# A gated linear-attention block: the Hadamard transform of gate's and up's input moved from the weights to the tokens

## The chip, the cores and the metric

One Trainium2 chip, one of its cores. The core has five engines that run beside each other, each in its own order: TensorE (PE, matmuls), VectorE (DVE), ScalarE (ACT), GpSimd (POOL) and SyncE (SP, which in this kernel issues nearly all DMAs). They meet through semaphores. The metric is the device time of one launch in microseconds; less is better. A profile is one execution taken by the hardware profiler; its times can be followed instruction by instruction.

## The reference

Input x is 8 batch elements of 512 tokens by 512 features, float32. Cut to what is computed:

```python
xn = layernorm(x)
# attention: q, k, v by 512x512 weights with bias; phi = elu + 1
ctx = phi(q) * cumsum(phi(k) * v, over tokens) / sqrt(32)
s   = ctx @ Wo.T + bo
# feed-forward, hidden size 2048; fwht = normalized Walsh-Hadamard transform
h   = fwht(xn * SU_ug) / 64
up, gate = (h @ W.T * (Wscale * 64) for W in (W_up, W_gate))
h   = fwht(silu(gate) * up * SU_dp) / 64
d   = h @ W_down.T * (Wscale_dp * 64)
out = x + s * silu(d)
```

The transform of a vector of 512 can be applied to the input, as written, or to the columns of the weights, which then take xn itself.

## The kernel before

**Tiles and pairs.** The eight batch elements are taken in four pairs p = 0 to 3. A pair's product is split by two in rows of the weights, in columns and in batch elements, and done with seven products of blocks instead of eight (`P1` to `P7`, a Strassen-like scheme): the tokens, the weights and the results each have seven "factors" or blocks. For pairs 1 to 3, gate and up are computed with two levels of the scheme (49 products of quarter blocks, `hidden_unit` and `block_product`), on second-level weight factors that pair 0 stored to DRAM (`inner_w`).

**Stages of a pair.** `attention` (k, v, q in two groups of heads), then four units u of the hidden layer (gate and up for 512 hidden columns, result `ho`), with the output projection `project_out` after unit 0; `down` in two halves, half 0 after unit 1, half 1 after unit 3. Half 0 writes its sums to tiles `dn` and stores them (`put_by`); half 1 fetches them and adds its own, gates, multiplies and writes out. `down` goes through `token_groups`: two groups g of tokens, products P1 and P7 first, then P2 (bank py), P6, P5, P3, P4. The sums of P2 for group 0 must be read by DVE (`output`, line 543) before P2 of group 1 can use the only `py` bank.

**Weights of gate and up.** In pair 0, `folded_w` (lines 919 to 955) loads a raw weight tile, runs four butterflies on DVE (lines 930 to 933), two matmuls with the 128x128 Hadamard matrix `had` on PE (line 939), scales by SU_ug on ACT while copying back (line 945), and forms the factors (`encode_weights`). There are 16 such tiles. Down's weights get their transform in the same pair: `butterflies_down`, `fold_down`, and then `first_half_down` for half 0, with `down_w` for half 1.

**Tokens.** Pair 0's tokens are normalized and transposed by PE (`transposed`) into `xo`, which holds the first-level factors of the pair. For later pairs, `normalized` normalizes an element by token on DVE during the pair before and stores it (`d_x`); `next_tokens` reads it back as 32x32 squares (`squares`), turns the squares with DVE's transpose, and forms the factors. `inner_tokens` and `inner_t3` add the second-level factors to the same `xo`, which attention, gate and up all use.

**What sets the order.** `at(place, fn)` puts a step on an agenda counted in places (one product of TensorE each); `advance` runs it. `later(us, fn)` puts work of DVE on a list, and `pace` issues entries of it behind each sum on DVE, up to a number of microseconds. `background` lowers the priority. A scheduler then fixes one order for each engine, and each engine, SP too, goes through its own strictly in order: an instruction that waits holds up everything behind it on that engine. Weights are streamed three tiles ahead through a pool of four (`wpool`); working tiles share a pool of six (`t8`), `ho` and `co` a pool of two (`hop`).

Of the kernel before, what the change touches and what calls it, by code (L numbers as in the profile page):

```python
# [10 lines left out]
ALU = mybir.AluOpType  # L11
# [10 lines left out]
def kernel(  # L22
# [26 lines left out]

    nc = tc.nc  # L50
# [14 lines left out]
    hop = ctx.enter_context(tc.tile_pool(name="hop", bufs=2))  # L65
# [53 lines left out]
    su_ug = const.tile([P, KD], F32, tag="su_ug", name="su_ug")  # L119
# [3 lines left out]
    def load_x(b, t=None, parts=1):  # L123
        if t is None:
            t = xin.tile([P, 3, 7, P], F32, tag="x", name=f"x_{b}")
            t = t.rearrange("p c s e -> p (c s e)")[:, : NT * D].rearrange("p (n d) -> p n d", n=NT)
        n = NT // parts
        for i in range(0, NT, n):
            nc.sync.dma_start(
                t[:, i : i + n], x[b, i * P : (i + n) * P, :].rearrange("(n p) d -> p n d", p=P)  # L130
            )
        return t
# [48 lines left out]


    def normalized(b):

        xt = load_x(b)
        d = dram.tile([L, D], F32, tag=f"d_x_{b}", name=f"d_x_{b}")
        kept[f"x_{b}"] = d

        def store():
            nc.sync.dma_start(d.rearrange("(n p) d -> p n d", p=P), xt)  # L190

        if b > 3:
            layernorm(b, xt)
            store()
            return
        mv = small.tile([P, NT, 2], F32, tag="mv", name=f"mv_{b}")
        rstd = small.tile([P, NT], F32, tag="rstd", name=f"rstd_{b}")

# [15 lines left out]

        def start():
            for t in range(NT):
                later(0.8, stats, t)
            later(0.3, root)
            for t in range(NT):
                later(0.6, scaled, t)  # L220
            later(0.0, store)

        at(12, start)

    def squares(b):


        if b % 2:
            z = t8.tile([P, KD, L], F32, tag="t", name=f"z_{b}")
        else:  # L230
            z = xin.tile([P, 3, 7, P], F32, tag="x", name=f"z_{b}")
            z = z.rearrange("p c s e -> p (c s e)")[:, : KD * L].rearrange("p (c t) -> p c t", c=KD)
        d = kept[f"x_{b}"].rearrange("(i t) (c j f) -> j t c i f", t=32, j=4, f=32)
# [4 lines left out]
    def next_tokens(b, xo):  # L238

        za, z = squares(b), squares(b + 1)  # L240

        def turned(place, z, h):

            for j in range(2):
                later(0.7, nc.vector.transpose, xo[:, place, j : j + 3 : 2, :], z[:, 2 * h + j])

        def less(o, a, b):
            later(1.2, nc.vector.tensor_tensor, xo[:, o, 0:4], xo[:, a, 0:4], xo[:, b, 0:4], ALU.subtract)

        turned(P1, za, 0)  # L250
        turned(P2, za, 1)

        def rest():
            turned(P7, z, 0)
            turned(P3, z, 1)
            less(P5, P7, P1)
            less(P6, P3, P5)
            less(P7, P3, P7)
            less(P4, P2, P6)

        at(10, rest)

# [3 lines left out]
    def transposed(b, xt, xo):  # L266
        s = b % 2
        for t in range(NT):
# [7 lines left out]
            else:  # L276
# [4 lines left out]
                nc.vector.tensor_tensor(o[:, P7], o[:, P3], b12, ALU.subtract)  # L281
        if s == 1:
            o = xo[:, :, 0:4]
            nc.vector.tensor_tensor(o[:, P4], o[:, P2], o[:, P6], ALU.subtract)

    def inner_tokens(xo):

        for o, a, b in ((P5, P7, P1), (P6, P3, P5), (P4, P2, P6)):
            later(2.0, nc.vector.tensor_tensor, xo[:, :, o], xo[:, :, a], xo[:, :, b], ALU.subtract)

    def inner_t3(xo, factors):
        for i in factors:
            nc.vector.tensor_tensor(xo[:, i, P7], xo[:, i, P3], xo[:, i, P7], ALU.subtract)
# [80 lines left out]
    def down_w(u, j):  # L374

        t = t8.tile([P, 2, 7, P], F32, tag="t", name=f"wd_{u}_{j}")
        w = by_factor(t)
        rows_w(w, wd_f, u + NU * j, NG)

        def encode():  # L380
            for o, a, b, op in (
                (P5, P7, P4, ALU.add), (P6, P5, P1, ALU.subtract), (P3, P2, P6, ALU.subtract), (P7, P1, P7, ALU.subtract)
            ):
                later(0.5, nc.vector.tensor_tensor, w[:, o], w[:, a], w[:, b], op)
            later(0.0, store)
# [56 lines left out]
    def group(name, ws, rhs, dst, then, bias=(None, None)):  # L442
# [24 lines left out]
        def output(i, s, p):  # L467
            pace(nc.vector.tensor_tensor(dst[i], s, p.rearrange("p a t -> p (a t)"), ALU.add), 1.7)  # L468
# [43 lines left out]
    def token_groups(name, n, tok, wts, dst, add=None, early=None, done=None, last=None):  # L512
# [29 lines left out]
        def output(o, p, a, s, g):  # L542
            pace(nc.vector.tensor_tensor(dst(a, s, g), o, p, ALU.add), 1.0)  # L543
# [78 lines left out]
    def block_product(name, w, x, out, add, done):  # L622
# [5 lines left out]
        def product(p, i, first):  # L628
            for lane in range(2):
                nc.tensor.matmul(  # L630
                    p[:, lane], w[:, lane, i, :], x[:, i, :],
# [171 lines left out]
    def hidden_unit(p, u, xo, ho, get_w, last):  # L803
# [4 lines left out]
        def outer(i, out, add=None, done=None):  # L808
            w = get_w("gu", (u, i))
            block_product(f"gu_{p}_{u}_{i}", w, xo[:, i], out, add, done)  # L810
# [108 lines left out]
    def folded_w(name, src, f):  # L919

        w = raw_w(f"{name}_{f}", src, 0, 2, 1, f * P, NG * P)
        places = (slice(P1, P7 + 1, 2), slice(P2, P4 + 1, 3))
        rs = []

        def butterflies():
            t = t8.tile([P, 2, 2, 2, 2, P], F32, tag="t", name=f"r_{name}_{f}")
            r2, r = t[:, 0], t[:, 1]
            rs.append(r)
            a, b = (w[:, :, place, :] for place in places)
            nc.vector.tensor_tensor(r2[:, 0], a, b, ALU.add)  # L930
            nc.vector.tensor_tensor(r2[:, 1], a, b, ALU.subtract)
            nc.vector.tensor_tensor(r[:, :, 0], r2[:, :, 0], r2[:, :, 1], ALU.add)
            nc.vector.tensor_tensor(r[:, :, 1], r2[:, :, 0], r2[:, :, 1], ALU.subtract)

        def fold():
            for b in range(2):
# [316 lines left out]
```

## Time and profile before

| | us |
|---|---|
| median of 3 runs (lowest, highest) | 1569.39 (1566.1, 1570.06) |
| the profiled execution's own time | 1565.26 |
| its span, first to last instruction | 1563.5 |
| PE busy in the stretches 0:50, 50:100, 100:200 | 41.8, 46.6, 92.0 |
| PE busy in 200:300, 300:400, 400:500 | 98.7, 96.8, 95.9 |
| PE busy in each 100 us from 500 to 1500 | 100.0 |
| DVE busy in 50:100, 100:200, 200:300 | 48.9, 81.9, 54.8 |
| DMA, mean share of 16 engines on the one queue | 51.8% |

Pair 0 takes the first 460 us or so, the other three some 365 each. "Busy" of an engine is the time in which it ran an instruction; matmuls overlap, so two that follow each other are closer than the duration of one. Rows of the timeline give start, duration, engine, line, operation, output and inputs, size and count, and in brackets how long the engine had been idle and what ended that.

### The profile page before, as it was taken

Reading aid. Unit: us, or ns where it says so; the run is one execution under the profiler, and the core shown is the slowest. Engines: PE = TensorE matmul, PEld = TensorE weight load, DVE = VectorE, ACT = ScalarE, POOL = GpSimd, SP = SyncE. Lnnn points to the kernel's source line nnn. Section 1 sums busy time; section 2 is a strip of 40 time slices with the busy share of each in tenths; the row PEclk is TensorE's granted clock in tenths of the full one; section 3 lists DMA queues with packets and bytes.
Section 4 is the critical chain, followed back from the end, with each engine's and each line's share of the span. In section 5 each row is a group of like instructions: output and inputs, shape, how many; then the busy total and the mean of one; then the engine's idle time right before and its main releaser. Section 6 shows DMA issues by size and latency. Waiting matters only on the chain.

```text
span 1563.5 us, 15520 instructions
## 1 busy us (share of the span) xinstructions
PE 1529.6 (98%) x5840; PEld 1105.7 (71%) x5840; DVE 953.9 (61%) x1336; ACT 419.8 (27%) x666; POOL 501.5 (32%) x286
## 2 busy tenths in 40 slices
PE   7989999999999999999999999999999999999998
PEld 4335546744584588888885488888886468888887
DVE  5898784469466674716676574725675476543673
ACT  5453340232114521112215431111212431111211
POOL 4532144014421252304612235301622226110731
PEclk9999999999999999999999999999999999999999
DMA  8244966566885344344575434335474233535462
GB/s 280 83 148 152 285 227 205 185 199 214 229 305 173 89 161 152 110 159 158 157 283 216 101 138 144 139 101 195 151 250 172 82 106 118 185 98 178 152 251 95
DMA packets 196682, 266.86 MB, mean 171 GB/s; under 512 B 56704, under 2 KB 155008, under 8 KB 192384
## 3 DMA queue, kind: packets, MB, share of 16 engines
q1 hardware_dynamic: 196464, 265.84, 51.8%
q8 instruction: 46, 0.75, 0.2%
q14 instruction: 28, 0.23, 0.0%
q10 hardware_dynamic: 144, 0.03, 0.0%
HBM read 189.83 MB, written 76.02 MB: 170 GB/s over the span
## 4 chain that ended last, share of the span: by engine, by line
PE 88%; DVE 4%; DMA 2%; POOL 2%; ACT 2%; issue 2%; SPq 0%; POOLq 0%; DVEq 0%; ACTq 0%
PE px_gu L630 19%; PE px_dn L528 13%; PE pz_gu L630 9%; PE pz_dn L528 6%; PE py_gu L630 5%; PE py_dn L528 4%; PE px_o L528 3%; PE px_up L452 3%; PE px_k L452 3%; PE px_v L452 3%; PE px_gate L452 3%; PE px_q L452 3%; PE pz_o L528 2%; PE pz_q L452 2%; PE pz_k L452 2%
## 5 line engine op out<-in xcount | busy, mean ns | idle before, releaser
L630 PE MATMUL px_gu<-xo,w_gu 128*128 128x256 f32 x1344 | 320.6, 380 | 0.0
L630 PEld LDWEIGHTS px_gu<-xo,w_gu 128*128 128x128 f32 x1344 | 254.7, 190 | 39.9 <-issue 3.6
L528 PE MATMUL px_dn<-w_down,ho 128*128 128x256 f32 x1024 | 228.5, 379 | 0.0
L528 PEld LDWEIGHTS px_dn<-w_down,ho 128*128 128x128 f32 x1024 | 194.5, 190 | 28.2 <-issue 2.1
L630 PE MATMUL pz_gu<-xo,w_gu 128*128 128x256 f32 x672 | 172.9, 380 | 0.0
L831 POOL TENSOR_TENSOR u<-u,v 128x1024 f32<-128x1024 f32 x24 | 56.1, 2359 | 354.2 <-DVE u L668 347.5
L630 PEld LDWEIGHTS pz_gu<-xo,w_gu 128*128 128x128 f32 x672 | 127.2, 190 | 18.4 <-DVE a L672 0.9
L528 PE MATMUL pz_dn<-w_down,ho 128*128 128x256 f32 x496 | 112.7, 380 | 2.7 <-POOL ho L300 2.7
L528 PEld LDWEIGHTS pz_dn<-w_down,ho 128*128 128x128 f32 x496 | 93.6, 190 | 17.9 <-POOL ho L300 3.5
L876 POOL TENSOR_TENSOR s<-s,d 128x512 f32<-128x512 f32 x30 | 40.4, 1346 | 152.8 <-ACT d L875 113.7
L716 POOL TENSOR_TENSOR v<-v,k 128x1024 f32<-128x1024 f32 x16 | 43.0, 2686 | 140.4 <-ACT v L691 112.7
L630 PE MATMUL py_gu<-xo,w_gu 128*128 128x256 f32 x336 | 86.2, 379 | 0.0
L630 PEld LDWEIGHTS py_gu<-xo,w_gu 128*128 128x128 f32 x336 | 63.9, 190 | 8.7
L793 POOL TENSOR_TENSOR ho<-g,u 128x512 f32<-128x512 f32 x8 | 12.5, 1557 | 164.6 <-DVE u L468 154.7
L835 POOL TENSOR_TENSOR v<-v,r 128x1024 f32<-128x1024 f32 x24 | 56.2, 2365 | 25.6 <-DVE r L668 25.6
L452 PE MATMUL px_v<-xo,w_v 128*128 128x512 f32 x128 | 60.8, 594 | 1.5 <-ACT sc_v L464 1.5
L875 ACT ACTIVATE d<-d 128x512 f32<-128x512 f32 x31 | 19.5, 630 | 158.3 <-DVE d L543 116.1
L452 PE MATMUL px_k<-xo,w_k 128*128 128x512 f32 x128 | 60.9, 597 | 1.1 <-ACT sa_k L464 1.0
L452 PE MATMUL px_gate<-xo,w_gate 128*128 128x512 f32 x128 | 59.7, 594 | 0.9 <-ACT sc_gate L462 0.9
L452 PE MATMUL px_q<-xo,w_q 128*128 128x512 f32 x128 | 60.1, 592 | 0.0
L452 PE MATMUL px_up<-xo,w_up 128*128 128x512 f32 x128 | 59.3, 592 | 0.0
L528 PE MATMUL px_o<-w_o,co 128*128 128x256 f32 x256 | 58.4, 379 | 0.0
(263 smaller groups left out, 2464.1 us busy)
## 6 DMA issues: line engine op xcount, KB each, us to landing
w_gu<-d_gu SPq DMA_DIRECT2D x84, 896.0 KB, 4.5
w_down<-d_down SPq DMA_DIRECT2D x56, 512.0 KB, 3.5
d_s<-o SPq DMA_DIRECT2D x8, 1024.0 KB, 4.4
d_d<-dn SPq DMA_DIRECT2D x8, 1024.0 KB, 7.6
d<-d_d SPq DMA_DIRECT2D x8, 1024.0 KB, 6.7
s<-d_s SPq DMA_DIRECT2D x8, 1024.0 KB, 7.9
y<-in_x_dram SPq DMA_DIRECT2D x8, 1024.0 KB, 7.8
out_dram<-y SPq DMA_DIRECT2D x15, 512.0 KB, 3.3
```

What stands on the lines that cost most here:

```text
L452: nc.tensor.matmul(p.rearrange("p a t -> p (a t)") if len(r.shape) == 2 else p, ws[k][:, i, :], r, start=(first and k == 0), stop=(k == n ...
L528: nc.tensor.matmul(p[:, c], t[:, (2 * g + c) * P : (2 * g + c + 1) * P], ws[i](k), start=(first and k == 0 and c == cs[0]), stop=(k == n - ...
L630: nc.tensor.matmul(p[:, lane], w[:, lane, i, :], x[:, i, :], start=(first and lane == 0), stop=True, skip_group_check=True,)
L716: nc.gpsimd.tensor_tensor(v[:, h], v[:, h], k[:, h], ALU.mult)
L793: nc.gpsimd.tensor_tensor(ho[:, P1], g[:, 0, 0], r[:, 0, 0], ALU.mult)
L831: nc.gpsimd.tensor_tensor(r[:, m], ru1[:, m], rv[:, m], ALU.add)
L835: nc.gpsimd.tensor_tensor(rv[:, m], rv[:, m], rr[:, m], ALU.add)
L875: nc.scalar.activation(d, d, AF.Silu)
L876: (nc.vector if final and (a, s) == (1, 0) else nc.gpsimd).tensor_tensor(r, r, d, ALU.mult)
```

## The change

Gate's and up's weights are no longer transformed. Their tiles are loaded raw and only get their factors (`hidden_w`). Instead there are two sets of tokens: plain ones for attention (`xa`) and transformed ones for gate and up (`xp`), each in a tile of `hop`, which has three now; the second-level factors move to a tile of their own (`xi`), whose space in pair 0 serves for down's weights (`rd`) and the scaled Hadamard matrices (`hads`).

- Pair 0: `first_transform` multiplies the factors of each of the two elements by `hads` on PE (four products), copies on ACT and does four butterflies on DVE.
- Pairs 1 to 3: `normalized` also stores the tokens times SU_ug (`times_scales`, POOL, then `d_xs`). In half 0 of down of the pair before, `transforms` reads both elements back and runs the full transform by token: nine levels of two steps (128x1024 each) for the odd element on DVE and for the even one on POOL (`transformed`), and stores the results (`d_xh`). During the next attention `hidden_tokens` reads them as squares, turns them and forms both levels of factors.
- The factor 1/sqrt(512) goes into gate's scale and `su_dp`; the preparation of down's weights starts two groups later; `first_half_down` uses `down_w`; the sums of down's half 0 release up to 5.0 us of listed work each instead of 1.0, those of `group` 2.2 instead of 1.7.

```diff
-    hop = ctx.enter_context(tc.tile_pool(name="hop", bufs=2))
+    hop = ctx.enter_context(tc.tile_pool(name="hop", bufs=3))
...
+    def normalized(b, delay=12):
+        t = xin.tile([P, 3, 7, P], F32, tag="x", name=f"x_{b}").rearrange("p c s e -> p (c s e)")
+        xt = t[:, : NT * D].rearrange("p (n d) -> p n d", n=NT)
+        su = t[:, NT * D : (NT + 1) * D]
+        load_x(b, xt)
+        nc.sync.dma_start(su, su_row.rearrange("o d -> (o d)").partition_broadcast(P))
...
+        def store():
+            put("x")
+            at(10, times_scales)
+        def times_scales():
+            for t in range(NT):
+                nc.gpsimd.tensor_tensor(xt[:, t], xt[:, t], su, ALU.mult)
+            put("xs")
...
+    def transformed(b, eng):
+        a, t = (t8.tile([P, NT, D], F32, tag="t", name=f"{n}_{b}") for n in ("xs", "xh"))
+        nc.sync.dma_start(a, kept[f"xs_{b}"].rearrange("(n p) d -> p n d", p=P))
+        d = dram.tile([L, D], F32, tag=f"d_xh_{b}", name=f"d_xh_{b}")
+        kept[f"xh_{b}"] = d
+        n = D.bit_length() - 1
+        def level(i, op):
+            x, y = ((a, t), (t, a))[i % 2]
+            x, y = (v.rearrange("p n (c t h) -> p (n c) t h", t=2, h=1 << i) for v in (x, y))
+            eng.tensor_tensor(y[:, :, op], x[:, :, 0], x[:, :, 1], (ALU.add, ALU.subtract)[op])
+            if i + 1 == n and op == 1:
+                nc.sync.dma_start(d.rearrange("(n p) d -> p n d", p=P), (a, t)[n % 2])
+        return [lambda i=i, op=op: level(i, op) for i in range(n) for op in range(2)]
...
+    def hidden_tokens(b, xp):
+        za = squares(f"xh_{b}", xin)
+        def first():
+            turned(xp, P1, za, 0)
+            turned(xp, P2, za, 1)
+            later(0.0, second)
+        def second():
+            z = squares(f"xh_{b + 1}", xin)
+            def rest():
+                turned(xp, P7, z, 0)
+                turned(xp, P3, z, 1)
+                outer_factors(xp)
+                inner_tokens(xp)
+            at(10, rest)
+        at(10, first)
...
+    def token_factors(name):
+        return new_h(name).rearrange("p m s t -> p (m s t)").rearrange("p (i n t) -> p i n t", i=7, n=4)
...
+    def first_transform(s, xa, xp):
+        t = t8.tile([P, KD, L], F32, tag="t", name=f"xh_{s}")
+        t2 = t8.tile([P, KD, L], F32, tag="t", name=f"xh2_{s}")
+        def product(c):
+            x = (xa[:, (P1, P2)[c // 2]] if s == 0 else (xp[:, P7], xa[:, P3])[c // 2])[:, c % 2 : c % 2 + 3 : 2, :]
+            p = ps.tile([P, 2, H], F32, tag="t", name=f"ph_{s}_{c}")
+            tc.keep_in_program_order(
+                nc.tensor.matmul(p, hads[:, c * P : (c + 1) * P], x, start=True, stop=True)
+            )
+            nc.scalar.copy(t[:, c], p.rearrange("p a t -> p (a t)"))
+        def butterflies():
+            places = slice(P1, P2 + 1) if s == 0 else slice(P7, P3 + 1)
+            u = t2.rearrange("p (h j) (i t) -> p j h i t", h=2, i=2)
+            for j, op in enumerate((ALU.add, ALU.subtract)):
+                later(1.2, nc.vector.tensor_tensor, t2[:, 2 * j : 2 * j + 2], t[:, 0:2], t[:, 2:4], op, soon=True)
+            for j, op in enumerate((ALU.add, ALU.subtract)):
+                later(1.2, nc.vector.tensor_tensor, xp[:, places, j : j + 3 : 2, :], u[:, 0], u[:, 1], op, soon=True)
+            if s == 1:
+                outer_factors(xp, soon=True)
+        for c in range(KD):
+            at(2 * c, lambda c=c: product(c))
+        at(2 * KD + 2, butterflies)
...
+    def inner_tokens(xp):
+        for o, a, b in (
+            (xi[:, :, P5 - P4], xp[:, :, P7], xp[:, :, P1]),
+            (xi[:, :, P6 - P4], xp[:, :, P3], xi[:, :, P5 - P4]),
+            (xi[:, :, 0], xp[:, :, P2], xi[:, :, P6 - P4]),
+            (xp[:, :, P7], xp[:, :, P3], xp[:, :, P7]),
+        ):
+            later(2.0, nc.vector.tensor_tensor, o, a, b, ALU.subtract)
...
+            pace(nc.vector.tensor_tensor(dst(a, s, g), o, p, ALU.add), 5.0 if n == 4 and add is None else 1.0)
...
-    def folded_w(name, src, f):
+    def hidden_w(name, src, f):
 
         w = raw_w(f"{name}_{f}", src, 0, 2, 1, f * P, NG * P)
-        places = (slice(P1, P7 + 1, 2), slice(P2, P4 + 1, 3))
-        rs = []
-        def butterflies():
-            t = t8.tile([P, 2, 2, 2, 2, P], F32, tag="t", name=f"r_{name}_{f}")
-            r2, r = t[:, 0], t[:, 1]
-            rs.append(r)
-            a, b = (w[:, :, place, :] for place in places)
-            nc.vector.tensor_tensor(r2[:, 0], a, b, ALU.add)
-            nc.vector.tensor_tensor(r2[:, 1], a, b, ALU.subtract)
-            nc.vector.tensor_tensor(r[:, :, 0], r2[:, :, 0], r2[:, :, 1], ALU.add)
-            nc.vector.tensor_tensor(r[:, :, 1], r2[:, :, 0], r2[:, :, 1], ALU.subtract)
-        def fold():
-            for b in range(2):
-                p = ps.tile([P, 2, 2, P], F32, tag="t", name=f"pw_{name}_{f}_{b}")
-                tc.keep_in_program_order(
-                    nc.tensor.matmul(
-                        p.rearrange("p j a e -> p (j a e)"), had,
-                        rs[0][:, b].rearrange("p j a e -> p (j a e)"), start=True, stop=True,
-                    )
-                )
-                for j in range(2):
-                    nc.scalar.activation(
-                        w[:, j, places[b], :], p[:, j], AF.Copy, scale=su_ug[:, 2 * b + j : 2 * b + j + 1]
-                    )
         def encode():
             encode_weights(nc.vector, w)
-            folded[name, f] = w
+            encoded[name, f] = w
             if f >= NU:
                 with background():
-                    inner_w(name, f - NU, folded[name, f - NU], w)
-        return w, [(6, butterflies), (5, fold), (9, encode)]
-    folded = {}
+                    inner_w(name, f - NU, encoded[name, f - NU], w)
+        return w, [(7, encode)]
...
+    hads = rd[:, 2 * NF * P + D : 2 * NF * P + 2 * D]
+    for c in range(KD):
+        nc.vector.tensor_scalar(hads[:, c * P : (c + 1) * P], had, col("su_ug", c), None, ALU.mult)
...
+        0: [lambda: first_transform(0, xa, xp)], 1: [lambda: normalized(2)], 2: [begin_down],
+        3: [lambda: first_transform(1, xa, xp), lambda: load_down(1)],
+        5: [lambda: nc.sync.dma_start(bo_r, bo.partition_broadcast(P))],
...
+    def transforms(p):
+        odd = transformed(2 * p + 3, nc.vector)
+        even = transformed(2 * p + 2, nc.gpsimd)
+        with background():
+            for step in even:
+                step()
+            for step in odd[:8]:
+                step()
+        for step in odd[8:]:
+            later(1.2, step)
...
+            xp = token_factors(f"xp_{p}")
+            hidden_tokens(2 * p, xp)
...
+        if p and more:
+            normalized(2 * p + 2)
...
+            if more and u == 0:
+                normalized(2 * p + 3)
             if u == 1:
+                if more:
+                    at(1, lambda p=p: transforms(p))
...
+            xa = token_factors(f"xa_{p + 1}")
+            next_tokens(2 * p + 2, xa)
```

## The prediction

> **What bounds the kernel now.** I read the busy row, then the slices, then PE's waits, then the stretches around the places that the change touches.
>
> ```profile
> PE 1529.6 (98%) x5840; PEld 1105.7 (71%) x5840; DVE 953.9 (61%) x1336; ACT 419.8 (27%) x666; POOL 501.5 (32%) x286
> PE   7989999999999999999999999999999999999998
> L939 PE MATMUL pw_gate<-r_gate,had 128*128 128x512 f32 x32 | 15.1, 594 | 3.2 <-DVE r_gate L933 3.2
> L939 PE MATMUL pw_up<-r_up,had 128*128 128x512 f32 x32 | 15.0, 592 | 0.0
> w_down<-d_down SPq DMA_DIRECT2D x56, 512.0 KB, 3.5
> ```
>
> TensorE is the bound: from 500 to 1500 us its stretches are 100% busy, and before that some 20 us of short waits are spread over the first pair. So each matmul that goes is worth its issue time, and each wait that is put on TensorE's own order costs in full. One matmul of the program is two records. In a run of them the spacing counts, not the 592 ns: x4 of 128x512 advance the clock by 1.72 us (0.43 each), x16 of 128x256 by 3.45 us.
>
> **What it removes.** The 64 fold records (last L939 rows above) go: 64 x 0.43 = 27.5 us. Eight products with `hads` come: 16 x 0.43 = 6.9. TensorE: **-20.6 us**. With the folds go the waits that PE had at them (3.2 on r_gate, 3.2 and 1.0 at the fold of down that stood behind them): **-7.4**. DVE loses the 64 butterflies L930 to L933 (26.1 + 26.0 us) and ACT 64 scaled copies (12.8 + 13.3), all beside TensorE; worth nothing more than the waits just counted.
>
> **Small additions in the first pair.** ACT: 4 copies of 0.37 and 8 of 0.58 us, in its gaps (3.06 us idle before sb_k). DVE: four 128x128 products for `hads` among the first layer norms, some 0.2 each by their width against the 0.55 of a 128x512 scale; 8 butterflies and 4 subtractions, 12 x 1.2 = 14.5 us, in the stretch 50 to 100 us where DVE was 48.9 of 50 busy and where the folds of two weights and one more step of down's fold leave. The first weight of down is now loaded behind the stores of gate's factors and a 1 MB load of xs. I take **+7** for all this, from 0 (all hidden) to 20 (the 14.5 on the path, the load 5 late).
>
> **Attention of the later pairs.** 8 transposes x 0.68 + 4 x 1.2 + 4 x 2.02 for the second set of factors, less the old 3 x 2.02 + 7 x 0.72: +7 us of DVE a pair. DVE is 65 of 100 us busy at 800:900 with TensorE at 100%, so 0; if that cover is gone, +22 in all. The eight 256 KB square loads a pair land in 5.0 us, on a DMA half idle: 0.
>
> **The transform by token, three times.** It sits in down's first half: 18 steps of 128x1024 on DVE for one batch element, 18 on POOL for the other, each with two SBUF inputs. In the half as it is, both are idle:
>
> ```profile
> 650.00:700.00 50.00, 50.00 (x233) 43.96 (x233) 13.12 (x16) 6.35 (x11) 0.00 (x0) 1.00 0.40 125
> 664.07 3.62 PE L528 MATMUL py_dn<-w_down,ho 128*128 128x256 f32 x16
> 667.52 3.62 PE L528 MATMUL px_dn<-w_down,ho 128*128 128x256 f32 x16
> 667.78 0.69 DVE L543 TENSOR_TENSOR dn<-sa_dn,py_dn 128x512 f32<-128x512 f32 x1 [7.95 <-PE py_dn L528]
> 670.98 3.62 PE L528 MATMUL py_dn<-w_down,ho 128*128 128x256 f32 x16
> 674.43 17.43 PE L528 MATMUL px_dn<-w_down,ho 128*128 128x256 f32 x80
> ```
>
> (The first row is the stretch 650 to 700: PE, PEld, DVE, ACT, POOL busy.) DVE 13 of 50, POOL none: 18 x 1.2 = 22 and 18 x 2.35 = 42 us seem to fit. But they don't run beside each other:
>
> ```profile
> 160.72 2.35 DVE L969 TENSOR_TENSOR rd<-rd 128x1024 f32<-128x1024 f32 x2
> 641.79 4.68 POOL L835 TENSOR_TENSOR v<-v,r 128x1024 f32<-128x1024 f32 x2 [2.13 <-DVE r L668]
> 198.21 2.13 POOL L298 TENSOR_TENSOR ho<-ho 128x512 f32<-128x512 f32 x1
> 199.73 3.90 DVE L93 TENSOR_TENSOR rd<-rd 128x1024 f32<-128x1024 f32 x2
> 200.30 2.24 POOL L300 TENSOR_TENSOR ho<-ho 128x512 f32<-128x512 f32 x1
> 202.51 2.25 POOL L299 TENSOR_TENSOR ho<-ho 128x512 f32<-128x512 f32 x1
> ```
>
> Alone, two DVE steps take 2.35 us and two POOL steps 4.68. Together, at 199.73, two DVE steps take 3.90, and POOL's 128x512 steps 2.24 instead of 1.26: each waits for the other's whole instruction, in turn. Add 1.13 (DVE) and 1.2 (POOL) alternately from 200.3 and every end in the rows comes out. The Trainium skill says so too (SBUF — State Buffer, Who interferes with whom): a DVE instruction with two SBUF inputs and a GpSimd one that reads SBUF contend, and the one that comes second blocks for the whole instruction. What a mean row would make of it: L969 over all its records is 1365 ns, so 8 steps are 11 us and nothing waits. By the rule, a 1024-wide DVE step behind a 1024-wide POOL step costs 1.13 + 2.3 = **3.4 us**, three times the mean; no row shows that pair for long, the alternation of the rows above decides, and I take 3.4. The first level's stride is 8 bytes; its price isn't in the trace. Bounds: the rows' prices, or POOL half as much again (+21 us a pair). I take the former.
>
> Two orders of the changed program then carry the wait to TensorE. (1) On DVE, 8 of the 18 steps stand ahead of the sum that frees the one py bank, and py_dn of the second token group waits for it. (2) On SP, the store of POOL's result (it waits for step 18) stands ahead of down's weight for P3, its weight for P4 and the next unit's; SP issues in order, so they all wait for POOL.
>
> Second pair, in the clock of before: POOL is free at 649.7 (v L822 ends). Until the sum, DVE has 3 encodings of ho, 8 steps and 2 more ho operations to do: 13 x 3.4 = 44 from 650.8, so the sum ends at 695.5; py_dn's second group, at 670.98 before, comes **24.5 us late**. From there four products (13.8 us) to P3 at 709.3. POOL's 18 steps end at 649.7 + 18 x 3.4 = 711; 0.4 to issue and 3.5 to land (row w_down above): P3 at 715 instead of 684.8. **+30 us**; the rest (P4's bank, DVE's last steps at 718) is in time. Third pair the same. First pair: POOL has ho's last product and three encodings as well (2.3 + 3 x 1.25), DVE four factors of up: POOL 47.5 + DVE's 21 turns x 1.13 = 71 us from 252, and 3.9 for the weight: P3 at 327.5 instead of 288.0, **+40** (its sum at 43 us delays it first, by 22). Together **+100**.
>
> Each of these stops is over 5 us long. After a stop of 3.2 us the trace shows
>
> ```profile
> 107.92 2.46 PE L988 MATMUL pwd<-rd,had 128*128 128x512 f32 x4 [3.16 <-ACT w_gate L945]
> 110.18 3.14 PE L452 MATMUL pz_gate<-xo,w_gate 128*128 128x512 f32 x4
> 113.16 1.88 PE L452 MATMUL px_gate<-xo,w_gate 128*128 128x512 f32 x4
> ```
>
> eight records from 107.92 to 113.16, 5.2 us for 3.4: 1.8 us to get back to speed. Six long stops: **+11**.
>
> **Sum** on the profiled execution's 1565.3 (span 1563.5): -20.6 - 7.4 + 7 + 100 + 11 = **1655 us**. The median of the runs is 4 us above that execution; within the rounding of this sum.
>
> **Rivals.**
> (a) The waits bite, as above: 1610 to 1690, chance 0.68.
> (b) DVE and POOL do not hold each other up in these steps, only SP's order bites. POOL then needs 18 x 2.34 = 42 us: done at 692, weight at 695.7 against 684.8, +11 twice; first pair 2.36 x 19 + 3.8 = 49 from 252, weight at 305 against 288, +17 to 19. 1565 - 21 + 41 + 5 = 1591. For it: strides may change the access; against: the same kinds of instructions alternate at 50, 71, 195 and 374 us. 0.17.
> (c) On the other side: the transforms end in time, because POOL starts them well before down does or its store waits behind nothing urgent. The point is POOL's last step at 681 in the clock of before (P3's weight less 3.9). To end there it must have begun at 639 alone, or at 620 in turns; its slot comes free only at 649.7. If it holds, the 20.6 and some of the 7.4 remain: 1545 (1537 to 1556). For it: TensorE is at 98% and really loses work. 0.12.
> (d) The two cancel, because the stop is short: 1561 to 1569. 0.03.
>
> About 0.3% (4.7 us) can be told from no change. **Chances:** faster 0.12, same 0.03, slower 0.85. Range: (a) with a tail cut above, down to (b): 1588 to 1690.
>
> **What would show it.** In the changed profile: no pw rows and 16 ph records; three dips of PE's digits in the slices of down's first half; DVE's L250 at 2 to 3.4 us instead of 1.2 and POOL's L250 at over 3; PE's longest waits "py_dn <- DVE dn" near 20 us and "px_dn <- DMA w_down" near 5 to 19. If L250 shows 1.2 and 2.35, (b); if PE's row stays at 9 throughout, (c) and the forecast is wrong. If the stops are there but the first pair before down is longer or shorter by over 10, the +7 is wrong.

## The result and the profile after

The changed kernel takes 1696.1 us (median of 4 runs, 1694.5 to 1697.8) against 1569.4 of the kernel before on the same chip: ratio 1.081, 95% interval 1.079 to 1.083. It is slower, as forecast, but by 127 us where 86 to 90 were forecast, and it lies 6 us above the forecast's range. The profiled execution took 1696.23 us, its span is 1694.5.

From the page of the changed kernel, the busy row, PE's slices (42.4 us each) with the granted clock, and two of the costliest groups:

```profile
PE 1544.3 (91%) x5792; PEld 1109.9 (66%) x5792; DVE 1117.0 (66%) x1372; ACT 397.9 (23%) x614; POOL 715.1 (42%) x364
...
PE   7879997399999899949999989977999999999998
...
PEclk9989998799999999989999999988999999999999
...
L250 POOL TENSOR_TENSOR xh<-xs 128x1024 f32<-128x1024 f32 x30 | 93.8, 3145 | 1.1
...
L250 DVE TENSOR_TENSOR xh<-xs 128x1024 f32<-128x1024 f32 x30 | 77.9, 2626 | 0.3
```

PE was at 9 nearly everywhere before. Now it has three holes, at 254 to 339, 720 to 762 and 1101 to 1186 us: the three first halves of down that carry the transform by token. The clock is lower in the same slices. The transform's steps show a mean of 3145 ns on POOL and 2626 on DVE. The small dips to 8 at 551 and 974 us are not in a first half of down; they will matter.

From PE's waits in the changed kernel (us in total, times, longest):

```profile
PE px_dn L613 <- DMA w_down<-d_down: 38.8, 4, 21.8
PE py_dn L613 <- DVE dn L628: 35.0, 3, 15.6
PE px_v L537 <- ACT sc_v L549: 8.5, 4, 6.2
...
PE pz_q L537 <- DVE q L553: 7.1, 1, 7.1
```

and the same two waits of attention in the kernel before:

```profile
PE pz_q L452 <- DVE q L468: 3.4, 1, 3.4
...
PE px_v L452 <- ACT sc_v L464: 1.5, 1, 1.5
```

The first two of the changed kernel are the waits that the prediction named. The third and fourth are stops of attention, longer than before, 6.2 and 7.1 us of them in the first pair. The 131 us between the spans are given here by stages, read from where PE's rows pass from one product to the next (in pair 0, products of down that stand among those of up are counted with down):

| stage, us | before | after | more |
|---|---|---|---|
| pair 0, up to the last product of up in unit 1 | 251.9 | 261.7 | 9.8 |
| pair 0, half 0 of down | 50.1 | 92.0 | 41.9 |
| pair 0, units 2 and 3, half 1 | 163.7 | 151.3 | -12.4 |
| pair 1, attention and unit 0 | 115.2 | 124.6 | 9.4 |
| pair 1, half 0 | 51.1 | 82.6 | 31.5 |
| pair 2, attention and unit 0 | 112.4 | 124.8 | 12.4 |
| pair 2, half 0 | 51.1 | 81.9 | 30.8 |
| pair 3, attention and unit 0 | 112.1 | 118.1 | 6.0 |
| all the rest | | | 1.5 |

Half 0 of pair 1 in the timeline of the changed kernel (start, duration, engine, line, operation, output and inputs, count, idle time before):

```profile
698.78 5.59 POOL L250 TENSOR_TENSOR xh<-xs 128x1024 f32<-128x1024 f32 x2
...
720.92 6.66 DVE L250 TENSOR_TENSOR xs<-xh 128x1024 f32<-128x1024 f32 x2
...
723.27 6.53 POOL L250 TENSOR_TENSOR xh<-xs 128x1024 f32<-128x1024 f32 x2
...
740.60 0.67 DVE L628 TENSOR_TENSOR dn<-sa_dn,py_dn 128x512 f32<-128x512 f32 x1
...
741.33 5.10 PE L613 MATMUL py_dn<-w_down,ho 128*128 128x256 f32 x16 [15.60 <-DVE dn L628]
...
752.72 3.33 POOL L250 TENSOR_TENSOR xh<-xs 128x1024 f32<-128x1024 f32 x1
...
756.08 0.37 SPq L252 DMA_DIRECT2D d_xh<-xh  x1
756.54 1.51 SPq L420 DMA_DIRECT2D w_down<-d_down  x2
...
762.62 5.72 PE L613 MATMUL px_dn<-w_down,ho 128*128 128x256 f32 x13 [5.83 <-DMA w_down<-d_down]
```

Two DVE steps take 6.66 us and two POOL steps 6.53 in the same time: they alternate. The sum `dn` runs at 740.60 and py_dn follows after a stop of 15.60. POOL's last step ends at 756.05, the store is issued at 756.08, down's last two weights behind it, and px_dn stops again.

In the first pair the three longest of TensorE's stops in half 0 are these:

```profile
267.63 8.13 PE L613 MATMUL px_dn<-w_down,ho 128*128 128x256 f32 x24 [5.91 <-DMA w_down<-d_down]
...
300.42 5.39 PE L613 MATMUL py_dn<-w_down,ho 128*128 128x256 f32 x16 [4.90 <-DVE dn L628]
...
337.95 8.84 PE L613 MATMUL px_dn<-w_down,ho 128*128 128x256 f32 x32 [21.78 <-DMA w_down<-d_down]
```

The first is for down's first weight, which SP issues only at 259.68, behind the two loads of `xs`; without these loads (e5, below) it is issued at 256.11 and the stop is 1.67.

### The profile page after: what moved, and what is told of

Same layout as the page of the kernel before. It is cut to its first block, busy times and chain, and to the rows that moved or that the text cites. A ratio compares the mean times of both kernels' runs of the same rounds, so it can differ in the third digit from the quotient of the medians.

```text
span 1694.5 us, 15526 instructions
## 1 busy us (share of the span) xinstructions
PE 1544.3 (91%) x5792; PEld 1109.9 (66%) x5792; DVE 1117.0 (66%) x1372; ACT 397.9 (23%) x614; POOL 715.1 (42%) x364
## 4 chain that ended last, share of the span: by engine, by line
PE 62%; DVE 13%; POOL 11%; DMA 6%; issue 3%; ACT 2%; SPq 1%; POOLq 0%; DVEq 0%; ACTq 0%
PE px_gu L715 14%; PE px_dn L613 9%; PE pz_gu L715 7%; PE pz_dn L613 4%; POOL xh L250 4%; PE py_gu L715 3%; PE px_o L613 3%; POOL xs L250 3%; PE px_v L537 2%; PE py_dn L613 2%; PE px_k L537 2%; PE px_q L537 2%; PE px_up L537 2%; PE pz_o L613 2%; PE px_gate L537 2%
## 5 line engine op out<-in xcount | busy, mean ns | idle before, releaser
L613 PE MATMUL px_dn<-w_down,ho 128*128 128x256 f32 x1024 | 239.3, 391 | 38.8 <-DMA w_down<-d_down 38.8
L715 PE MATMUL px_gu<-xp,w_gu 128*128 128x256 f32 x672 | 172.9, 380 | 7.0 <-DMA w_gu<-d_gu 3.9
L715 PE MATMUL px_gu<-xi,w_gu 128*128 128x256 f32 x672 | 174.3, 381 | 3.2 <-ACT sb_gu L723 2.0
L715 PEld LDWEIGHTS px_gu<-xp,w_gu 128*128 128x128 f32 x672 | 127.2, 190 | 27.6 <-issue 5.5
L715 PEld LDWEIGHTS px_gu<-xi,w_gu 128*128 128x128 f32 x672 | 126.6, 190 | 26.4 <-ACT sb_gu L723 5.0
L250 POOL TENSOR_TENSOR xh<-xs 128x1024 f32<-128x1024 f32 x30 | 93.8, 3145 | 1.1
L715 PE MATMUL pz_gu<-xi,w_gu 128*128 128x256 f32 x336 | 86.8, 381 | 3.0 <-DVE a L746 3.0
L715 PE MATMUL pz_gu<-xp,w_gu 128*128 128x256 f32 x336 | 86.5, 380 | 0.0
L715 PE MATMUL py_gu<-xp,w_gu 128*128 128x256 f32 x336 | 86.2, 379 | 0.0
L250 DVE TENSOR_TENSOR xh<-xs 128x1024 f32<-128x1024 f32 x30 | 77.9, 2626 | 0.3
L250 POOL TENSOR_TENSOR xs<-xh 128x1024 f32<-128x1024 f32 x24 | 74.9, 3140 | 0.9
```

What stands on the lines that cost most here:

```text
L250: eng.tensor_tensor(y[:, :, op], x[:, :, 0], x[:, :, 1], (ALU.add, ALU.subtract)[op])
L613: nc.tensor.matmul(p[:, c], t[:, (2 * g + c) * P : (2 * g + c + 1) * P], ws[i](k), start=(first and k == 0 and c == cs[0]), stop=(k == n - ...
L715: nc.tensor.matmul(p[:, lane], w[:, lane, i, :], x(i), start=(first and lane == 0), stop=True, skip_group_check=True,)
```

## The experiments

Runs are one execution each with its profile, beside the kernel before (1566 to 1569 us in these series), where nothing else is said. Seven executions of the kernel before lie between 1565.1 and 1571.1 us, so a difference of a few us between two totals says little; the stages say more. Even there, the end of unit 1 of the first pair lies between 261.6 and 263.4 us in the changed kernel and e1 to e3, which do the same work up to it.

### e1: two steps of the transform kept

```diff
+        odd = odd[-2:]
+        even = even[-2:]
```

> The changed kernel with 16 of the 18 steps of each transform by token left out (only the last level, two steps, is kept for each element; the loads of xs and the stores of xh stay), so gate and up of pairs 1 to 3 get tokens that are not transformed. By stages of the two traces the three first halves of down hold 43 + 32 + 31 = 105 us of the difference. Theory (the steps make the stops there): TensorE has no stop over 3 us in any half 0, and the time is 1696 - 105 = 1591. Rival (the stops come from what else moved into half 0: the transfers, six tiles of t8 taken, listed work of 5 us behind each sum): half 0 stays 20 us or more longer than before, time over 1620. Either way what is left above the time before, 22 us at 1591, is not the transform's but that of the first pair and of the attentions.

Measured 1621.8. The half 0 stages of pairs 1 and 2 took 60.1 and 58.7 us: 22 us of each excess gone, 8 to 9 left. The run was not the zero it was meant to be. In it the two kept DVE steps stand ahead of u's sum and begin only when POOL's two have ended (676.48: px_dn after 5.85 us for `u`), and both stores stand on SP ahead of down's weights that are still to come. So the rival's number came out, by way of the kept steps, and a run with no steps at all was needed: e5.

### e2 and e3: one engine alone

e2 has only the second of the two lines above, e3 only the first.

> The changed kernel with 16 of POOL's 18 steps left out and DVE's 18 kept (even elements of pairs 1 to 3 not transformed). Theory (DVE and POOL hold each other up, and the DVE steps ahead of the sum cost because of it): DVE's step falls from 2.8 to 1.2 us, the wait of py_dn for DVE goes from 35 us to under 5, and the time is within 6 us of the run without steps: 1591 to 1597. Rival (the eight DVE steps ahead of the sum make the stop by their place in DVE's order, whatever POOL does): py_dn still waits 10 us or more in each half, time 1615 to 1640.

> The changed kernel with 16 of DVE's 18 steps left out and POOL's 18 kept (odd elements of pairs 1 to 3 not transformed). Theory: POOL's step falls from 3.14 to 2.35 us; py_dn does not wait for DVE any more; the store of POOL's result still stands ahead of down's weight for P3, which comes 11 us late in pairs 1 and 2 and 17 late in pair 0 : 1591 + 39 = 1630, and px_dn waits for w_down in all three halves. Rival (POOL is slow by its own strides or counts, 3.1 us also alone): the weight is 25 or more late, time 1665.

Measured 1626.9 (e2) and 1651.4 (e3). The steps' rows (min/median/max ns), first of e2, then of e3:

```profile
L250 DVE TENSOR_TENSOR xs<-xh x24: 1215/1218/3364, 269.3 to 1095.7; 128x1024 f32<-128x1024 f32 x24
```

```profile
L250 POOL TENSOR_TENSOR xs<-xh x24: 1894/2353/3313, 278.9 to 1118.9; 128x1024 f32<-128x1024 f32 x24
```

Alone, a DVE step takes 1.22 us and a POOL step 2.35. Sixteen more DVE steps per pair cost 5 us over e1 in all, sixteen more POOL steps 30; in e2 py_dn no longer waits for DVE at all. Both together cost 1696 - 1622 = 74. What is above 35, 39 us, is the price of running them beside each other, and it is the lower bound: in e3 POOL's first eight steps of a pair still take 2.8 to 3.3 us beside ho's encodings and the two DVE steps. POOL alone also delays the weights (px_dn waits for w_down 24.2 us, pz_dn 13.7); 30 us came out where 39 were expected.

### e4: SP's order alone

```diff
-            if i + 1 == n and op == 1:
-                nc.sync.dma_start(d.rearrange("(n p) d -> p n d", p=P), (a, t)[n % 2])
+    def stores(*fns):
+        with tc.issue_after(last_down[0].ins):
+            for fn in fns:
+                fn()
...
+        later(0.0, stores, store_even, store_odd)
```

> The changed kernel with only the two stores of xh moved on SP's queue, behind all seven weights of down's half 0. Theory (two waits, the lock on DVE's order and SP's order, of which the longer shows): px_dn no longer waits for w_down (38.8 us before), py_dn waits for DVE as before (35 us or somewhat more), half 0 keeps about 20 us of its excess in each pair: time 1650 to 1665. Rival (SP's order carries the whole excess; py_dn's stop is a part of it): half 0 back near its old length, time 1600. Second rival (nothing gained, since DVE's and POOL's last steps end past the half and the stores now hold up the weights of the next unit): 1685 to 1696, with px_gu or px_gate waiting for its weights at the start of unit 2.

Measured 1674.4. PE's waits:

```profile
PE py_dn L621 <- DVE dn L636: 36.7, 3, 15.8
PE px_gate L545 <- ACT sb_gate L555: 10.4, 2, 9.3
```

py_dn waits as long as before; of px_dn's 38.8 us, 5.6 are left. Half 0 of pairs 1 and 2 falls from 82 to 75: SP's order was worth 7 there and the lock the other 24. In pair 0, half 0 lost 18, but units 2 and 3 and half 1 took 14 more: gate's raw weights are now the loads behind the two stores (issued at 329.99, right after them), and px_gate waits 3.7 us for them and soon after 9.3 for ACT. Hence 22 us in all, where 31 to 46 were expected.

### e5: no transform by token

```diff
-                    at(1, lambda p=p: transforms(p))
+                    for b in (2 * p + 2, 2 * p + 3):
+                        kept[f"xh_{b}"] = kept[f"xs_{b}"]
```

> The changed kernel with the transform by token left out as a whole in pairs 1 to 3: no steps, no loads of xs for them, no stores of xh; the attention reads the scaled tokens xs in place of xh. In the run with two steps kept, half 0 stayed 8 to 11 us longer than before. Theory (those two steps, which stand ahead of u's sum on DVE and wait for POOL, and their stores on SP, made that rest): half 0 takes 51 us in pairs 1 and 2 as before, and the time is 1696 - 105 = 1591. Rival (other things moved into half 0 hold it up): half 0 stays at 58 to 60, time 1615 to 1622.

Measured 1586.2, half 0 at 51.1 us in pairs 1 and 2. The transform by token costs 110 us, 104 of them in the three half 0 stages. The other 17 us above before are left: pair 0 and the attentions.

### e7: all of the transform, on DVE

```diff
-        even = transformed(2 * p + 2, nc.gpsimd)
+        even = transformed(2 * p + 2, nc.vector)
...
+        for *steps, store in (even, odd):
+            for step in steps:
+                later(1.2, step)
+            later(0.0, stores, store)
...
+            ins = sub(eng, P4, P2, P6)
+            if last:
+                pace(ins, 7.0)
```

> The changed kernel, complete, with both transforms on DVE and none on POOL: six steps behind the last encoding of ho, five behind each sum of half 0, the stores of xh behind down's weights on SP, and the normalization moved as in the run with parts. Theory (lock and orders made the stops): steps 1.2 us, no stop over 4 us in half 0, whose three stages are within 5 us of before; time 1575 to 1590, that is 105 to 120 us less than the changed kernel, but not below before because of the attention and the first pair. Rival (36 steps on DVE, 43 us, are more than half 0 has room for, 37 us): unit 2 starts late, 10 us or more in each pair, time 1605 to 1620.

Measured 1595.8, with the whole transform done. Its steps, and the stretch of half 0 of pair 1 (PE, PEld, DVE, ACT, POOL busy, then clock and DMA):

```profile
L250 DVE TENSOR_TENSOR xs<-xh x48: 1212/1218/1227, 286.0 to 1092.1; 128x1024 f32<-128x1024 f32 x48
```

```profile
656.00:707.00 51.00, 51.00 (x238) 44.84 (x237) 45.83 (x46) 8.20 (x13) 3.84 (x2) 1.00 0.47 135
```

Twice as many DVE steps as in the changed kernel, and PE is busy for 51.00 of 51. Half 0 takes 51.1 us in pairs 1 and 2. The 36 steps are handed out behind the sums, few enough that the next sum is not late, DVE is 46 of 51 busy, and what is over runs into unit 2 without a stop. The total is 9.5 us above e5. But e7 also has the layer norms where e6 puts them and reaches the end of unit 1 3.8 us before e5, so the transform itself costs 9.5 to 13 us, of which 8.9 are the wait of pair 0's down for its first weight, behind the loads of `xs`. e7 changes engine, place and SP's order at once. e2 shows that the old place alone costs next to nothing on one engine; both engines with good places and late stores were not run.

### e8: the kernel before without the fold

```diff
-        return w, [(6, butterflies), (5, fold), (9, encode)]
+        return w, [(9, encode)]
```

> The kernel before with only the fold of gate's and up's weights left out (their four butterflies, two products and scaled copies), so gate and up see weights that are not transformed. It measures the gain that the change could have at most. Theory: 64 records of 0.43 us and the 7.4 us of waits at them: 1569 - 35 = 1534. Rival (other work is late next where the folds waited, as DVE is 98% busy at 50 to 100 us and the first pair's end of down's preparation is bound to it): only the issue time, 1542, or less gain.

Measured 1531.5: the fold is worth 37.6 us against the run of before beside it, and 33.8 between the two profiles' spans. The two parts of pair 0 take 235.6 and 146.7 us in place of 251.9 and 163.7.

### e6, e9: the attentions

e6 (with the inner factors left out after pair 1) and e9 (on e5, without the scaling):

```diff
-        0: [lambda: first_transform(0, xa, xp)], 1: [lambda: normalized(2)], 2: [begin_down],
+        0: [lambda: first_transform(0, xa, xp)], 2: [begin_down], 7: [lambda: normalized(2)],
...
-            normalized(2 * p + 2)
+            normalized(2 * p + 2, 30)
...
+                if b == 2:
+                    inner_tokens(xp)
```

```diff
-            at(10, times_scales)
```

> The changed kernel with two edits outside half 0, to be read stage by stage. The normalization of the even element is moved: in pair 0 from the attention to after it, in pairs 1 and 2 by 18 places (some 15 us) later, off the end of the attention. And the second-level factors of the transformed tokens are formed only in pair 1; in pairs 2 and 3 they are left out (the old ones are used). Theory (attention's excess is DVE work at its end: 6 us by the four 2 us factor operations, and 3 to 6 by the layer norm with its two table loads on ACT; the first pair's by the early layer norm and POOL's scaling): attention of pair 1 falls from 124.6 to 118, of pair 2 from 124.8 to 113, of pair 3 from 118.1 to 112; the first down comes 10 us earlier; time 1660. Rival (the excess comes from the squares' transfers and their waits on SP's queue): no attention changes by more than 2 us, time 1685 or more.

> The run without the transform by token, and in addition POOL's scaling by SU and the second store (xs) left out; the layer norms stay where the change puts them. Gate and up of pairs 1 to 3 then see the plain tokens. Theory (the scaling, its wait for the first store, its 1.3 us instructions stretched to 1.7 to 2.2 beside DVE's, and the store of xs on SP ahead of the next unit's weights make what pairs 1 and 2 have over pair 3): attention of pairs 1 and 2 from 124.5 to 118, the first pair up to its half 0 by 5 us or more, time 1586 - 18 = 1568. Rival (the layer norm at the end of the attention does it, by its 6 us on DVE and two table loads on ACT): attention of pairs 1 and 2 stays at 122 or more, time 1580 or more.

Measured 1696.9 (e6): nothing gained. Attention took 124.6, 123.7 and 114.2 us in pairs 1, 2, 3. Moving the layer norm by 18 places does nothing; leaving out the four inner factors is worth about 1 us in pair 2 and 2 to 4 in pair 3 (116.4 to 118.1 in the other runs). In pair 0 the output projection comes 10.7 us earlier, and all but 1.4 of it is lost again by the end of unit 1. My theory of e6 fell.

e9 measured 1583.3. Attention of pairs 1 and 2: 119.9 us both, against 124.3 and 124.6 in e5. So POOL's scaling and its second store cost 4.5 us in each. In the changed kernel (timeline of pair 1):

```profile
588.21 0.37 SPq L193 DMA_DIRECT2D d_x<-x  x1
...
593.56 5.85 POOL L217 TENSOR_TENSOR x<-x 128x512 f32<-128x512 f32 x3 [12.43 <-DMA d_x<-x]
...
601.91 0.37 SPq L193 DMA_DIRECT2D d_xs<-x  x1
602.37 1.52 SPq L412 DMA_DIRECT2D w_gu<-d_gu  x2
```

POOL sits idle for 12.43 us until the first store has landed (issued at 588.21), three steps that take 1.26 each alone take 5.85 beside DVE's, and the second store then stands on SP ahead of weights of gate and up. The total of e9 fell by only 3 us, since down's weights came late in its pair 0 (half 0 at 55.4).

### e10, e11: two complete versions

e10 is e7 with the scaling as one more DVE step in half 0 (`eng.tensor_tensor(a, a, su.unsqueeze(1).to_broadcast([P, NT, D]), ALU.mult)`), no scaling on POOL, no second store, and the layer norms of pairs 1 and 2 after unit 0. e11 adds to e10:

```diff
+        later(0.0, lambda: early.append(squares(f"xh_{b}", xin)))
...
-        at(10, first)
+        first()
```

> The complete kernel with both transforms on DVE, and the scaling by SU moved into them: one more DVE step of 2.3 us on the tokens read back in half 0, no scaling on POOL, no second store; in pairs 1 and 2 both layer norms come after unit 0, as in the kernel before. Theory (scaling and early layer norm make the difference of pairs 1 and 2 from pair 3): their attention falls from 124.6 to 117 or 118, pair 0 loses its wait for down's weight (8.9), half 0 stays at 51 to 53; time 1596 - 14 - 9 = 1573. Rival (the squares and the factors of the second set, not the layer norm, fill DVE at the attention's end): attention stays at 122 or more, time 1585 or more.

> The run before this one, complete, and in addition the squares of the transformed tokens are loaded in half 1 of down of the pair before and turned from the attention's first place on, so that the second set's 20 us on DVE fall where DVE is a third busy and not at the attention's end. Theory (it is the place of this DVE work, not its amount, that costs the 4 to 6 us that also pair 3 has): attention of all three pairs near 113, time 1573 - 15 = 1558, below before. Rival (its amount: TensorE's sums wait for DVE wherever it stands): attention stays at 117, time 1570 to 1575, no faster than before.

e10: 1583.2, 10 above what was expected, attention at 120.0, 119.9 and 118.1; it is the fastest complete version that I found with tokens transformed, and slower than before (1566.4, the highest of 7 runs 1571.1). e11: 1604.1, ratio to before 1.022 (1.017 to 1.027). Its attentions fell to 118.1, 118.2 and 114.9, but the stage of units 2 and 3 and half 1 of down grew from 133 to 143 us in pairs 1 and 2: the early loads of squares stand on SP's queue ahead of down's last three weights, and px_dn waits for them (20.3 us over the run).

### e12, e13, e14: the first pair

e12 drops both `first_transform` entries of the plan and gives `xa` to gate and up of pair 0; e13 drops the entry below, and pair 1 takes element 3 twice; e14 has both.

```diff
-        0: [lambda: first_transform(0, xa, xp)], 1: [lambda: normalized(2)], 2: [begin_down],
+        0: [lambda: first_transform(0, xa, xp)], 2: [begin_down],
```

> The changed kernel with the first pair's transform left out (eight products with hads, their copies, eight butterflies, the factors of the second set), so gate and up of pair 0 read the plain tokens xa. Read at the first pair: the first product of down begins at 267.6 us in the changed kernel; before, without the 8 us of down's products that came earlier there, at 251.6. Theory (the 14.5 us of these DVE steps lie on the path, as DVE is busy without a gap from 80 to 110 us): 6.9 us of TensorE and 8 to 12 of stops go, first product of down at 249 to 253. Rival (the steps are hidden, only the products count): 260. Total time of the run 1696 less the same amount.

> The changed kernel without the layer norm and the scaling of element 2 in the first pair's attention (left out: pair 1 takes element 3 twice). Moving this work behind the attention had brought the output projection 10 us earlier and down no earlier. Theory (it is the amount of work on DVE, POOL, SP and the one xin tile that costs, wherever it stands in the first pair): left out, down's first product comes 8 to 12 us earlier, at 256 to 260. Rival (it is filled by other work that was waiting, as DVE's end of down's preparation binds the pair): 264 or later.

> The changed kernel with both left out, the first pair's transform and element 2's layer norm and scaling. Theory (two additions to one overfull stretch of DVE): the gains add, down's first product at 238 to 243, which is about where the kernel before has it without its folds (235). Rival (what is left is the later start of down's preparation, by two groups, and the 512 KB of down's weights formed at the end): 248 or later, and the wait of down for its weights is there.

Times 1690.7, 1682.7, 1680.1. The end of up in unit 1, with down's earlier products (8 us in e12 and e14) taken off, as in the table above: 263.3, 248.5 and 251.6 us against 261.7. The last product of up in unit 1, first of the changed kernel, then of e13:

```profile
259.74 1.98 PE L537 MATMUL pz_up<-xp,w_up 128*128 128x512 f32 x4
```

```profile
246.53 1.98 PE L537 MATMUL pz_up<-xp,w_up 128*128 128x512 f32 x4
```

So the first pair's own transform costs nothing that can be seen by then (without it the fold of down waits 8.0 us for ACT), which neither the theory nor the rival of e12 had, and the layer norm with the scaling of element 2 costs 13.2. In e13 the two stops of attention are gone or short:

```profile
PE pz_q L537 <- DVE q L553: 3.1, 2, 2.9
```

The wait for sc_v, 6.2 us in the changed kernel, has no row there. The gains do not add, against e14's theory; its rival fits, down waits 4.3 us for its weights there. The stretch seems bound by whichever of several chains is late, and not by a sum of DVE work.

## Why the prediction was right, and where it failed

**Right: what happens in half 0.** The sum of its three stages was forecast at +100 and 11 for getting back to speed, measured at 104. Pair by pair: +40 and +30, with 1.8 a stop, against 41.9, 31.5 and 30.8. The alternation is as worked out, 3.4 us forecast for a DVE step and 3.3 found (6.66 for two). e2 and e5 show that without POOL's steps DVE's cost next to nothing, e4 that the lock carries 24 of 31 us in pairs 1 and 2 and SP's order the rest. Within that sum py_dn's stop in pair 1 was put at 24.5 and was 15.6, with 3.6 before it for `u`. In the first pair the total is right in part by luck: py_dn was to be 22 late and stopped for 4.9, and 5.9 of the 41.9 are the wait for down's first weight, which the forecast had among the +7 ("the load 5 late").

**Right: what goes.** -20.6 with -7.4, or 34.9 for the fold without the new products; e8 measured 33.8 to 37.6. Rival (b), no lock, is excluded by e2 and e3. Rival (c), no stop at all, is what e7 comes to in pairs 1 and 2, with both transforms on DVE and their stores behind the weights. The changed kernel does not do it.

**Wrong: the term "Small additions in the first pair", +7.** It priced the first pair's own transform and some loads. The changed kernel reaches the end of unit 1 26.1 us later than e8, where 6.9 for the products and the +7 were forecast: over by 12, which is the forecast's own sign that the +7 is wrong. What the term left out is the layer norm with its scaling. Element 2's came from unit 1 into the attention and element 3's from behind unit 1 into it, so the stretch holds two where it held one. Each has 15 operations on DVE and ACT, four on POOL, four DMAs, and holds the one `xin` tile; the forecast counted a load. Leaving out element 2's gained 13.2 us (e13). Its place within the stretch matters less: e6 put it behind the attention and kept 1.4. Which of its parts costs the time was not found, and how the other 12.9 us divide stays open too, since leaving out the first pair's transform shortened nothing (e12). A further 4.6 us are in units 2, 3 and half 1 (151.3 against e8's 146.7). There the trace has short stops at gate's sums, 2.3 us for ACT and 1.3 for DVE, where e8 has 0.3; what made them late was not traced.

**Wrong: the term "Attention of the later pairs", 0 (22 if cover is gone).** Measured +27.8. The cover was read from a mean of 100 us, DVE 65 of 100. These are stretches of pair 1's attention in the changed kernel (length, then PE, PEld, DVE, ACT, POOL busy, clock, DMA share, GB/s):

```profile
510.00:520.00 10.00, 10.00 (x25) 4.38 (x24) 1.45 (x3) 3.02 (x5) 0.00 (x0) 1.00 1.06 271
...
560.00:570.00 10.00, 10.00 (x25) 4.44 (x24) 10.00 (x9) 5.59 (x7) 0.14 (x1) 1.00 0.34 118
570.00:580.00 10.00, 8.04 (x24) 4.17 (x23) 8.91 (x11) 2.31 (x4) 6.38 (x2) 1.00 0.27 92
...
590.00:600.00 10.00, 7.63 (x32) 5.54 (x32) 9.09 (x10) 4.80 (x7) 6.44 (x4) 1.00 0.48 164
```

and the last 20 us of the same attention in the kernel before:

```profile
520.00:530.00 10.00, 10.00 (x25) 4.49 (x24) 5.09 (x7) 5.70 (x7) 0.76 (x1) 1.00 0.28 93
530.00:540.00 10.00, 10.00 (x30) 5.42 (x29) 6.04 (x6) 2.65 (x4) 4.81 (x2) 1.00 0.27 92
```

DVE has 1.5 of 10 to do early and 9 to 10 late, where it had 5 to 6 before, and PE loses time from where DVE is full: the second set of squares is loaded only when the first has been turned, so its factors meet the end of the attention. The DMAs, taken as half idle, are full while squares are loaded (1.06 at 510 to 520), though TensorE lost nothing there. Of pair 2's 12.4 us, 4.5 are the scaling (e9); pair 3, which has no next pair to prepare, has 6.0 (4.3 in some runs), by elimination from the second set, of which e11's early loads took 3 and e6's missing factors 2 to 4. Some 2 us of pairs 1 and 2 stay open: with both layer norms after unit 0 (e10), they were still there.

The sum then reads: 1655, and 18 for pair 0 (13.2 and 4.6, the rest of the first stretch taken as forecast), 29 for the attentions and the rest of the pairs, less 7 in half 0: 1695. The forecast failed by what it priced at nothing or too low, not by the waits that it worked out. No run points to a version with transformed tokens that beats the kernel before: what e8 shows as the most to be had, 34 to 38 us, is more than taken back. In the best of them, e10, this is by 6.9 us of products, some 15 more in pair 0 up to down, 8 behind that, 5 to 8 in each attention, and 3 elsewhere.

## What to carry to other kernels

Count a step that moves into a stretch by its whole list of instructions on each engine and queue, and look for its cover in 10 us stretches at the place where its inputs let it run, not in a mean. Two engines that hold each other up can cost more together than one of them with all the work: 36 steps on one engine, handed out behind the sums that others need and with late stores, cost 9.5 to 13 us where 18 and 18 cost 110. And on an in-order DMA queue, a store that waits for compute, or a load made early, belongs behind the weights that are needed next.

## What was not expected of the hardware

- The stride has no price on DVE: in e7's pair 1 the two steps of the first level, which read every second element, take 2.35 us together, those of the last levels the same (median of all 1218 ns).
- The lock spares the sums that read PSUM: beside POOL's steps, `dn` took 0.67 us in the changed kernel as elsewhere, where a step with both inputs in SBUF went from 1.22 to 3.3. A sum is late because it stands behind such steps.
- A stop costs more than itself: in half 0 of pair 1 the listed waits are 15.6 + 5.8 + 3.6 = 25.0 us, and the stage is 31.5 longer. After the 15.6 us stop sixteen records of py_dn took 5.10 us where they take 3.62. The granted clock was 0.86 over that half.
- Leaving out 16 of 18 steps is not leaving out the transform: two steps a side in the wrong place (e1) cost 35.6 us more than none (e5), about three times what 36 in the right place cost.
